# Four later modulation vectors of a two-layer transformer kernel: computed as four strips, turned in blocks, placed by sixteen transfers

## The chip, the cores and the metric

The kernel runs on one core of one Trainium2 chip. The time is device time in microseconds (us) of one execution. Three runs of the kernel before gave 2197.56, 2198.17 and 2198.8 us; their median is 2198.17 us. The core has a matrix engine (TensorE, called PE in the profile; its weight loads are PEld), a vector engine (VectorE, DVE), a scalar engine (ScalarE, ACT), a general engine (GpSimd, POOL) and a queue engine (SyncE, SP) that here issues all data transfers. Each engine takes its instructions in the order of the program and waits on semaphores for the others.

## The reference

Sixteen sequences x of 256 tokens by 256 features pass through two transformer layers, all in float32. Each layer has self-attention, cross-attention on a context, and a feed-forward part, each on a normalized input that is scaled and shifted by vectors computed from a condition of 256 features per sequence. These vectors are the modulations:

```python
def _adaln(x, c, lw, lb, gw, gb, bw, bb):          # layer 0
    g = (c @ gw + gb)[:, None, :]
    bt = (c @ bw + bb)[:, None, :]
    return _ln(x, lw, lb) * (1.0 + g) + bt
...
mod = jax.nn.silu(time_emb) @ Wmod + bmod          # layer 1, time_emb is the same condition
sh1, sc1, sh2, sc2, sh3, sc3 = jnp.split(mod, 6, axis=-1)
h = _ln(x, ln1_w, ln1_b) * (1 + sc1[:, None, :]) + sh1[:, None, :]
```

Layer 0 has two modulations (one shared by its two attentions, one for the feed-forward part), layer 1 has three. Each is a product of 16 conditions by a 256 x 512 weight: shift and scale, 256 features each.

## The kernel before

**Phases and jobs.** Six phases run one after another (self-attention, cross-attention and feed-forward of layer 0, then the same of layer 1). Each has 16 jobs, one per sequence `b`. An attention job has two steps `s`, a feed-forward job four. The order of every engine's instructions is that in which the Python code emits them (`manual_schedule`), so what stands in a step's code is also the order in each engine's queue; buffers are handed out by tile pools, which add the waits for a buffer's earlier readers. The main loop is at L901.

**A layer-0 attention step.** PE computes queries and keys of the next step (L82; for cross-attention also L502) into banks 0 to 3 of its accumulator. DVE multiplies them by the cosine and sine tables (`m`, L523), two tiles for each half: one under the tag `m0` and one under `m1`, two buffers each. POOL combines them to rotated queries and keys (`qk`, L531). PE multiplies these to scores (L566): first the half that goes into banks 0 to 3, then the half that goes into banks 4 to 7. ACT takes exponentials (`pr`, L578). DVE sums these (`both` L587, `squares` L593, `rows` L600). PE multiplies them with the values (L635, into banks 4 and 5), and ACT copies the products out (`raw`, L642). POOL divides by the sums (`raw`, L624) and makes the combinations for a product with seven instead of eight blocks (`folded`, L733). In the second step of a job PE forms the output of the previous job from these (`finish_folded`, banks 4 and 5) and DVE adds it to x (L747 to L754). DVE then normalizes a later job (`xh` L335, `blocks` L345), and its block transposes travel through DRAM (`turned` L350, `fetched` L360).

**Modulations.** The five products are called a1, a2 (layer 0) and b1, b2, b3 (layer 1). a1 and a2 use `modulation` (L180): eight products with a 128 x 128 weight block as the stationary operand and the 16 columns of `condT` as the moving one (L186), which leaves features on partitions, as `factors` (L165) needs them. `factors` are five small DVE instructions (L173 to L177) on 128 x 32 elements. a1 is made before the first job. a2 is made at `b == 2`, `s == 1` of the cross-attention phase (L923, L985), in the middle of the next step's rotary work, and its factors follow at once. b1, b2 and b3 are made at jobs 2, 5 and 8 of layer 0's feed-forward phase (L960) by `modulation_turned` (L192): the condition is the stationary operand (16 columns), the whole 256 x 512 weight passes in two products of 512 columns (L198). The result has conditions on partitions; POOL zeroes a 32 x 512 tile (L202), ACT copies the result into it (L203), DVE transposes it in 32 x 32 blocks (L205, tile `blocks`, tag `m1`; the tile `flat` has tag `m0`), and four transfers put the blocks on their partitions (L208, tile `turned`). The factors are made one job later (`at["mod"]()`, in step 3 of jobs 3, 6 and 9).

Of the kernel before, what the change touches and what calls it, by code (L numbers as in the profile page):

```python
# [10 lines left out]
F32 = mybir.dt.float32  # L11
# [5 lines left out]
P = 128  # L17
N = 256
D = 256
# [5 lines left out]
KC = D // P  # L25
# [18 lines left out]
def fast(ctx: ExitStack, tc: tile.TileContext, a: dict, out: bass.AP, flag):  # L44
# [4 lines left out]
    nc = tc.nc  # L49
    NB = a["x"].shape[0]  # L50
    assert NB >= 11

    const = ctx.enter_context(tc.tile_pool(name="const", bufs=1))
    resid = ctx.enter_context(tc.tile_pool(name="resid", bufs=1))
    wpool = ctx.enter_context(tc.tile_pool(name="wpool", bufs=2))
    work = ctx.enter_context(tc.tile_pool(name="work", bufs=2))
# [7 lines left out]
    def bank(i, *inner):  # L64

        flat = banks[:, i, :]
        if len(inner) == 1:
            return flat[:, 0 : inner[0]]
        return flat[:, 0 : inner[0] * inner[1]].rearrange("p (a n) -> p a n", n=inner[1])
# [34 lines left out]
    row_of, n_rows = {}, 0  # L104
# [17 lines left out]

    cond = work.tile([NB, D], F32, tag="m1", name="cond")
    nc.sync.dma_start(out=cond, in_=a["cond_1024"])
    condT = const.tile([P, 2, KC, NB], F32, name="condT")

    def transpose_condition(s, src):
        pc = bank(5 + s, KC, NB)
        for c in range(KC):
            nc.tensor.transpose(pc[:, c, :], src[:, c * P : (c + 1) * P], ident[:NB, :NB])  # L130
        nc.vector.tensor_copy(condT[:, s], pc)

    def idle_products(n):

# [5 lines left out]
    def condition():  # L140

        sig = work.tile([NB, D], F32, tag="inv", name="sig")
        nc.scalar.activation(sig, cond, AF.Sigmoid)
        soon = stat.tile([NB, 1], F32, tag="ve", name="soon")
        nc.scalar.activation(soon, cond[:, 0:1], AF.Exp)
        silu = work.tile([NB, D], F32, tag="inv", name="silu")
        idle_products(1)
        transpose_condition(0, cond)
        nc.vector.tensor_mul(silu, sig, cond)
        idle_products(1)  # L150
        transpose_condition(1, silu)
        idle_products(2)
        pr = bank(4, n_rows)
        nc.tensor.transpose(pr, rows, ident[:n_rows, :n_rows])
        return pr

    def load_modulation(shift_w, scale_w, name, between=None):
        w = wpool.tile([P, KC, 2, D], F32, tag="mod", name=f"mod_{name}", bufs=1)
        nc.sync.dma_start(out=w[:, :, 0, :], in_=shift_w.rearrange("(c p) m -> p c m", p=P))
        if between is not None:  # L160
            between()
        nc.sync.dma_start(out=w[:, :, 1, :], in_=scale_w.rearrange("(c p) m -> p c m", p=P))
        return w

    def factors(name, pm, ln_w, ln_b, shift_b, scale_b):  # L165


        factor = stat.tile([P, KC, NB], F32, tag="fac", name=f"fac_{name}", bufs=4)
        addend = stat.tile([P, KC, NB], F32, tag="add", name=f"add_{name}", bufs=4)
        ln_w, ln_b, shift_b, scale_b = (  # L170
            cols[:, c : c + KC].unsqueeze(2).to_broadcast([P, KC, NB]) for c in (ln_w, ln_b, shift_b, scale_b)
        )
        nc.vector.tensor_tensor(addend, pm[:, 1], scale_b, ALU.add)  # L173
        nc.vector.scalar_tensor_tensor(factor, addend, 1.0, ln_w, ALU.add, ALU.mult)
        nc.vector.scalar_tensor_tensor(addend, addend, 1.0, ln_b, ALU.add, ALU.mult)
        nc.vector.tensor_tensor(addend, addend, shift_b, ALU.add)
        nc.vector.tensor_tensor(addend, pm[:, 0], addend, ALU.add)  # L177
        return factor, addend

    def modulation(name, at, w, *vectors):  # L180

        pm = bank(at, 2 * KC, NB).rearrange("p (s c) b -> p s c b", s=2)
        for s in range(2):
            for m in range(KC):
                for k in range(KC):
                    nc.tensor.matmul(  # L186
                        pm[:, s, m, :], w[:, k, s, m * P : (m + 1) * P], condT[:, 0, k, :],
                        start=(k == 0), stop=(k == KC - 1),
                    )
        return factors(name, pm, *vectors)  # L190

    def modulation_turned(name, at, w, *vectors):  # L192


        assert NB <= 32
        pm = bank(at, 2 * D)[0:NB]
        for k in range(KC):
            nc.tensor.matmul(  # L198
                pm, condT[:, 1, k, :], w[:, k].rearrange("p s m -> p (s m)"), start=(k == 0), stop=(k == KC - 1)
            )  # L200
        flat = work.tile([32, 2 * D], F32, tag="m0", name=f"flat_{name}")
        nc.gpsimd.memset(flat, 0.0)  # L202
        nc.scalar.copy(flat[0:NB], pm)  # L203
        blocks = work.tile([32, 2 * KC, 4, 32], F32, tag="m1", name=f"blocks_{name}")
        nc.vector.transpose(blocks.rearrange("p s q b -> p (s q b)"), flat)  # L205
        turned = work.tile([P, 2, KC, NB], F32, tag="inv", name=f"turned_{name}")
        for q in range(4):
            nc.sync.dma_start(  # L208
                out=turned[32 * q : 32 * q + 32].rearrange("p s c b -> p (s c) b"), in_=blocks[:, :, q, 0:NB]
            )  # L210
        return lambda: factors(name, turned, *vectors)

    def layer0_modulation(i, between=None):
        w = load_modulation(a[f"L0_xcond_b{i}_w"], a[f"L0_xcond_g{i}_w"], f"a{i}", between)
        return lambda at: modulation(
            f"a{i}", at, w,
            *(row_of[f"L0_xcond_{n}"][0] for n in (f"ln{i}_w", f"ln{i}_b", f"b{i}_b", f"g{i}_b")),
        )

    def layer1_modulation(i):  # L220
        at = 2 * (i - 1) * D
        w = load_modulation(
            a["L1_xcond_Wmod"][:, at : at + D], a["L1_xcond_Wmod"][:, at + D : at + 2 * D], f"b{i}"
        )
        c = row_of["L1_xcond_bmod"][0] + at // P
        return lambda at: modulation_turned(
            f"b{i}", at, w, row_of[f"L1_xcond_ln{i}_w"][0], row_of[f"L1_xcond_ln{i}_b"][0], c, c + KC
        )


# [559 lines left out]
    def count_outside():  # L790
# [10 lines left out]
    phases = [  # L801
        {"layer": 0, "kind": "attn", "cross": False, "load": lambda part: load_layer0_attention("sa", part, load_first),
         "mod_load": lambda: layer0_modulation(1, lambda: load_x(0))},
        {"layer": 0, "kind": "attn", "cross": True, "load": lambda part: load_layer0_attention("ca", part), "mod_load": None},
        {"layer": 0, "kind": "ffn", "cross": False, "mod_load": lambda: layer0_modulation(2),
         "load": lambda part: load_ffn("L0_xcond_ff_w1", "L0_xcond_ff_w2", "L0_xcond_ff_b1", "L0_xcond_ff_b2", "a", part)},
        {"layer": 1, "kind": "attn", "cross": False, "load": load_layer1_self, "mod_load": lambda: layer1_modulation(1)},
        {"layer": 1, "kind": "attn", "cross": True, "load": load_layer1_cross, "mod_load": lambda: layer1_modulation(2)},
        {"layer": 1, "kind": "ffn", "cross": False, "mod_load": lambda: layer1_modulation(3),
         "load": lambda part: load_ffn("L1_xcond_W1", "L1_xcond_W2", "L1_xcond_b1", "L1_xcond_b2", "b", part)},  # L810
    ]
# [18 lines left out]
    for p, ph in enumerate(phases):  # L830
        for b in range(NB):
            job = {"phase": ph, "p": p, "layer": ph["layer"], "kind": ph["kind"], "cross": ph["cross"], "b": b,
                   "key": f"{p}_{b}", "index": len(jobs), "qk": {}, "pr": {}, "turns": [], "raw": [], "parts": [], "halves": [],
                   "last": p == len(phases) - 1}
# [66 lines left out]
    for i, (j, s) in enumerate(steps):  # L901
        job = jobs[j]
        ffn, layer0 = job["kind"] == "ffn", job["layer"] == 0
# [17 lines left out]
            load_phase(job["p"] + 1, "first")  # L921
        if layer0 and not ffn and s == 1 and job["b"] == 2:
            make_mod = phases[job["p"] + 1]  # L923

        if ffn and layer0 and job["b"] in (2, 5, 8):
            at = phases[3 + job["b"] // 3]
# [4 lines left out]
        if ffn and layer0 and job["b"] in (3, 6, 9) and s == 3:  # L931
            at = phases[2 + job["b"] // 3]
# [84 lines left out]
        else:  # L1017
            then = attention(i + 1, 1)
            at = 4 * s
# [639 lines left out]
```

## Time and profile before

| quantity | value |
|---|---|
| median of three runs | 2198.17 us |
| the profiled execution's own time | 2198.01 us |
| its span in the profile | 2196.1 us |
| PE busy | 2181.5 us (99%) |
| DVE busy | 1669.3 us (76%) |
| POOL busy | 1072.3 us (49%) |
| ACT busy | 838.2 us (38%) |
| four transfers of one modulation (L208), issue | 2.56 us (b1), 3.55 us (b2), 2.54 us (b3) |

The span begins with the first instruction and ends with the last; about 1.9 us of the execution's time lie outside it. In a timeline each line gives the start, the duration of the group, the engine, the line of the code, the operation, output and inputs, shapes and the number of records. One float32 product shows as two records on PE. "SPq" is the time in which SP issues a transfer, not the time the data takes. Idle time before a group is given in brackets with what ended it.

### The profile page before, as it was taken

Reading aid. Unit: us, or ns where it says so; the run is one execution under the profiler, and the core shown is the slowest. Engines: PE = TensorE matmul, PEld = TensorE weight load, DVE = VectorE, ACT = ScalarE, POOL = GpSimd, SP = SyncE. Lnnn points to the kernel's source line nnn. Section 1 sums busy time; section 2 is a strip of 40 time slices with the busy share of each in tenths; the row PEclk is TensorE's granted clock in tenths of the full one; section 3 lists DMA queues with packets and bytes.
Section 4 is the critical chain, followed back from the end, with each engine's and each line's share of the span. In section 5 each row is a group of like instructions: output and inputs, shape, how many; then the busy total and the mean of one; then the engine's idle time right before and its main releaser. Section 6 shows DMA issues by size and latency. Waiting matters only on the chain.

```text
span 2196.1 us, 110711 instructions
## 1 busy us (share of the span) xinstructions
PE 2181.5 (99%) x50469; PEld 1437.0 (65%) x50469; DVE 1669.3 (76%) x3119; ACT 838.2 (38%) x1306; POOL 1072.3 (49%) x1036
## 2 busy tenths in 40 slices
PE   9999999999999999999999999999999999999998
PEld 5656656656656666666666668787656656557887
DVE  6877777777787999989898876664777777777654
ACT  3323323323323333333333332334666666663222
POOL 3766566566557767676776752221323232222220
PEclk9999999999999999999999999999999999999999
DMA  6210111110132221212212033221222232223221
GB/s 192 49 37 23 27 37 23 28 37 22 31 89 64 71 60 35 59 41 45 56 37 60 23 74 87 52 45 29 62 43 42 52 95 59 62 52 85 61 62 37
DMA packets 307974, 117.77 MB, mean 54 GB/s; under 512 B 244308, under 2 KB 290728, under 8 KB 307368
## 3 DMA queue, kind: packets, MB, share of 16 engines
q1 hardware_dynamic: 307496, 110.61, 21.5%
q8 instruction: 396, 6.49, 1.3%
q14 instruction: 82, 0.67, 0.1%
HBM read 77.14 MB, written 33.29 MB: 50 GB/s over the span
## 4 chain that ended last, share of the span: by engine, by line
PE 92%; DVE 2%; POOL 2%; DMA 1%; issue 1%; SPq 1%; ACT 0%; DVEq 0%; POOLq 0%; ACTq 0%
PE banks L82 60%; PE banks L566 15%; PE banks L635 9%; PE banks L651 5%; PE banks L502 1%; PE banks L469 1%; POOL raw L624 1%; DVE m L523 1%; POOL qk L531 1%; DMA spread<-sums_seen 0%; POOL folded L733 0%; DMA turned<-blocks 0%; SPq L615 0%; DVE both L587 0%; SPq L350 0%
## 5 line engine op out<-in xcount | busy, mean ns | idle before, releaser
L578 ACT ACTIVATE pr<-banks 128x1024 f32<-128x1024 f32 x576 | 487.6, 938 | 414.3 <-PE banks L566 209.5
L531 POOL TENSOR_TENSOR qk<-m,m 128x512 f32<-128x512 f32 x256 | 347.0, 1376 | 292.5 <-DVE m L523 190.7
L523 DVE TENSOR_TENSOR m<-banks,rope 128x512 f32<-128x512 f32 x512 | 324.1, 679 | 87.1 <-POOL qk L531 83.2
L587 DVE TENSOR_TENSOR both<-pr 128x512 f32<-128x512 f32 x256 | 227.9, 903 | 101.4 <-ACT pr L578 101.2
L642 ACT COPY raw<-banks 128x512 f32<-128x512 f32 x128 | 75.0, 587 | 468.5 <-PE banks L635 461.8
L566 PE MATMUL banks<-qk 32*64 32x256 f32 x8192 | 241.3, 378 | 2.9 <-DVE x L750 2.0
L635 PE MATMUL banks<-pr,v 128*32 128x256 f32 x4096 | 233.2, 379 | 0.0
L566 PEld LDWEIGHTS banks<-qk 32*64 32x64 f32 x8192 | 185.4, 131 | 62.9 <-issue 23.0
L701 ACT ACTIVATE g<-banks,cols 128x256 f32<-128x256 f32 x256 | 106.9, 470 | 288.3 <-PE banks L82 274.9
L635 PEld LDWEIGHTS banks<-pr,v 128*32 128x32 f32 x4096 | 133.1, 110 | 88.5 <-ACT pr L578 0.7
L624 POOL TENSOR_TENSOR raw<-raw,spread 128x512 f32<-128x512 f32 x128 | 164.6, 1318 | 25.4 <-DMA spread<-sums_seen 23.2
L82 PE MATMUL banks<-folded_w,folded 128*32 128x128 f32 x5856 | 175.1, 273 | 0.4 <-POOL folded L733 0.3
L82 PEld LDWEIGHTS banks<-folded_w,folded 128*32 128x32 f32 x5856 | 162.5, 110 | 1.5 <-POOL folded L733 1.5
L593 DVE STREAM_TRANSPOSE squares<-both 128x1024 f32<-128x1024 f32 x128 | 159.4, 1246 | 4.4
L600 DVE TENSOR_REDUCE rows<-squares 128x32 f32<-128x1024 f32 x128 | 155.5, 1215 | 2.2
L686 POOL TENSOR_TENSOR oT<-oT,spread 128x256 f32<-128x256 f32 x64 | 45.7, 735 | 209.9 <-DVE spread L685 209.9
L327 POOL TENSOR_TENSOR rstd<-ve,neg_half 128x2 f32<-128x2 f32 x95 | 75.1, 790 | 144.0 <-DVE ve L325 140.7
L651 PE MATMUL banks<-pr,wide_v 128*32 128x256 f32 x2048 | 134.4, 379 | 1.1 <-ACT pr L578 1.1
L82 PE MATMUL banks<-hT,wk_sa 128*32 128x256 f32 x2048 | 134.9, 381 | 0.1
L420 POOL TENSOR_TENSOR x<-x,bo_b 128x256 f32<-128x256 f32 x96 | 73.1, 781 | 126.1 <-DVE xh L335 126.1
L82 PE MATMUL banks<-hT,wq_sa 128*32 128x256 f32 x2048 | 134.0, 379 | 0.0
L82 PE MATMUL banks<-hT,wq_ca 128*32 128x256 f32 x2048 | 133.9, 379 | 0.0
(157 smaller groups left out, 3669.6 us busy)
## 6 DMA issues: line engine op xcount, KB each, us to landing
turned<-blocks SPq DMA_DIRECT2D x380, 64.0 KB
fetched<-turned SPq DMA_DIRECT2D x380, 64.0 KB
spread<-sums_seen SPq DMA_DIRECT2D x128, 128.0 KB
x<-in_x SPq DMA_DIRECT2D x16, 256.0 KB
fetched_c<-turned_c SPq DMA_DIRECT2D x64, 64.0 KB
cT<-in_ctx_turned SPq DMA_DIRECT2D x16, 256.0 KB
out<-x SPq DMA_DIRECT2D x16, 256.0 KB
ctx<-in_ctx SPq DMA_DIRECT2D x16, 192.0 KB
```

What stands on the lines that cost most here:

```text
L82: nc.tensor.matmul(out[cut], lhsT[:, cut], rhs, start=start, stop=stop)
L523: nc.vector.tensor_tensor(m, pq, rope[:, s : s + 1, :].to_broadcast([P, 2, N]), ALU.mult)
L531: nc.gpsimd.tensor_tensor(r, x, y, (ALU.subtract, ALU.add)[out])
L566: nc.tensor.matmul(banks[64 * g : 64 * g + 64, at + h, t * N : (t + 1) * N], lhs, rhs, start=(half == 0), stop=(half == 1 or job["layer"] ...
L578: nc.scalar.activation(pr[:, one], sc[:, one], AF.Exp, scale=0.125 if job["layer"] == 0 else 0.25)
L587: nc.vector.tensor_tensor(job["both"][:, 2 * p : 2 * p + 2, :], pr[:, :, 0, :], pr[:, :, 1, :], ALU.add)
L593: nc.vector.transpose(job["squares"].rearrange("p b k -> p (b k)"), job.pop("both").rearrange("p h n -> p (h n)"))
L600: nc.vector.tensor_reduce(job["rows"][:, u, :], job.pop("squares"), AX.X, ALU.add)
L624: nc.gpsimd.tensor_tensor(part, part, spread[:, u : u + 1, :].to_broadcast([P, 2, N]), ALU.mult)
L635: nc.tensor.matmul(o[32 * h : 32 * h + 32, half, :], v[:, t, col : col + 32], prs[h // 2][:, h % 2, t, :], start=(t == 0), stop=(t == NT - 1),
L651: nc.tensor.matmul(o[32 * h : 32 * h + 32], v[:, t, 4 * c + h, 32 * e : 32 * e + 32], prs[h // 2][:, h % 2, t, :], start=(t == 0), stop=(t ...
L701: nc.scalar.activation(g[:, c, :], ph[:, c, :], AF.Gelu, bias=column(w["b1"], 2 * u + c))
```

## The change

All modulations but a1 are made by a new form of `modulation_turned`. `condT` is held with 32 columns, the last 16 zero. The product is cut into four pieces of 128 weight columns (shift and scale, two chunks each), and each piece goes to its own 32 partitions of the accumulator: eight products of 32 stationary and 128 moving columns instead of two of 16 and 512. The result is then a full 128 x 128 tile, so the zeroing on POOL falls away; ACT copies 128 x 128 elements, DVE transposes 128 x 128 elements in 32 x 32 blocks, and each of the sixteen blocks is put in place by a transfer of its own (32 partitions by 16 elements) instead of four blocks by one. a2 now goes this way too, at the same place in the step; its factors move from that place to the beginning of `b == 3`, `s == 1`, one job later. `condT` is zeroed once on POOL at the start.

```diff
-    condT = const.tile([P, 2, KC, NB], F32, name="condT")
+    assert NB <= 32
+    condT = const.tile([P, 2, KC, 32], F32, name="condT")
+    nc.gpsimd.memset(condT, 0.0)
...
-        nc.vector.tensor_copy(condT[:, s], pc)
+        nc.vector.tensor_copy(condT[:, s, :, 0:NB], pc)
...
-    def modulation_turned(name, at, w, *vectors):
-        assert NB <= 32
-        pm = bank(at, 2 * D)[0:NB]
+    def modulation_turned(name, of, at, w, *vectors):
+        pm = bank(at, P)
         for k in range(KC):
-            nc.tensor.matmul(
-                pm, condT[:, 1, k, :], w[:, k].rearrange("p s m -> p (s m)"), start=(k == 0), stop=(k == KC - 1)
-            )
-        flat = work.tile([32, 2 * D], F32, tag="m0", name=f"flat_{name}")
-        nc.gpsimd.memset(flat, 0.0)
-        nc.scalar.copy(flat[0:NB], pm)
-        blocks = work.tile([32, 2 * KC, 4, 32], F32, tag="m1", name=f"blocks_{name}")
-        nc.vector.transpose(blocks.rearrange("p s q b -> p (s q b)"), flat)
+            for g in range(4):
+                nc.tensor.matmul(
+                    pm[32 * g : 32 * g + 32], condT[:, of, k, :], w[:, k, g // KC, g % KC * P : (g % KC + 1) * P],
+                    start=(k == 0), stop=(k == KC - 1),
+                )
+        flat = work.tile([P, P], F32, tag="m0", name=f"flat_{name}")
+        nc.scalar.copy(flat, pm)
+        blocks = work.tile([P, 4, 32], F32, tag="m1", name=f"blocks_{name}")
+        nc.vector.transpose(blocks.rearrange("p q b -> p (q b)"), flat)
         turned = work.tile([P, 2, KC, NB], F32, tag="inv", name=f"turned_{name}")
         for q in range(4):
-            nc.sync.dma_start(
-                out=turned[32 * q : 32 * q + 32].rearrange("p s c b -> p (s c) b"), in_=blocks[:, :, q, 0:NB]
-            )
+            for g in range(4):
+                nc.sync.dma_start(
+                    out=turned[32 * q : 32 * q + 32, g // KC, g % KC, :], in_=blocks[32 * g : 32 * g + 32, q, 0:NB]
+                )
         return lambda: factors(name, turned, *vectors)
 
     def layer0_modulation(i, between=None):
...
-        return lambda at: modulation(
+        make = modulation if i == 1 else lambda name, *rest: modulation_turned(name, 0, *rest)
+        return lambda at: make(
...
+        if layer0 and not ffn and s == 1 and job["b"] == 3:
+            late_mod = phases[job["p"] + 1]
+            if late_mod["kind"] == "ffn":
+                late_mod["mod"] = late_mod["mod"]()
```

`modulation` (for a1) reads `condT[:, 0, k, 0:NB]` instead of `condT[:, 0, k, :]`, and `layer1_modulation` passes `of = 1`.

More of the change, by code (lines that the diff above doesn't have):

```diff
@@ L186, in modulation @@
                     nc.tensor.matmul(
-                        pm[:, s, m, :], w[:, k, s, m * P : (m + 1) * P], condT[:, 0, k, :],
+                        pm[:, s, m, :], w[:, k, s, m * P : (m + 1) * P], condT[:, 0, k, 0:NB],
                         start=(k == 0), stop=(k == KC - 1),
@@ L226, in layer1_modulation @@
         return lambda at: modulation_turned(
-            f"b{i}", at, w, row_of[f"L1_xcond_ln{i}_w"][0], row_of[f"L1_xcond_ln{i}_b"][0], c, c + KC
+            f"b{i}", 1, at, w, row_of[f"L1_xcond_ln{i}_w"][0], row_of[f"L1_xcond_ln{i}_b"][0], c, c + KC
         )
```

## The prediction

> **What bounds the kernel now.** I read the busy times, the slices and the chain of waits first. The page says:
>
> ```profile
> span 2196.1 us, 110711 instructions
> PE 2181.5 (99%) x50469; PEld 1437.0 (65%) x50469; DVE 1669.3 (76%) x3119; ACT 838.2 (38%) x1306; POOL 1072.3 (49%) x1036
> DVE  6877777777787999989898876664777777777654
> PE 92%; DVE 2%; POOL 2%; DMA 1%; issue 1%; SPq 1%; ACT 0%; DVEq 0%; POOLq 0%; ACTq 0%
> ```
>
> PE sets the time, but around slices 13 to 22 (cross-attention of layer 0, where a2 is made) DVE is as full as PE, and its in-order queue can stop PE. So I read two stretches of the timeline. First PE in the feed-forward phase, at the same product of successive jobs:
>
> ```profile
> 1351.28 1.99 PE L82 MATMUL banks<-w_a,folded 128*32 128x128 f32 x63
> 1364.30 1.99 PE L82 MATMUL banks<-w_a,folded 128*32 128x128 f32 x63
> 1378.82 0.40 PE L82 MATMUL banks<-w_a,folded 128*32 128x128 f32 x6
> 1392.06 1.99 PE L82 MATMUL banks<-w_a,folded 128*32 128x128 f32 x63
> ```
>
> A job takes 13.02 us (1364.30 - 1351.28); the two that hold b2 take 27.76, so b2 costs PE 27.76 - 26.04 = 1.72 us, all of it in the time. Then the step in which a2 is made:
>
> ```profile
> 787.16 1.96 PE L186 MATMUL banks<-condT,mod_a 128*128 128x16 f32 x16
> 789.05 0.64 PE L82 MATMUL banks<-cT,wk_ca 128*32 128x256 f32 x8
> 790.13 2.56 POOL L531 TENSOR_TENSOR qk<-m,m 128x512 f32<-128x512 f32 x2 [0.72 <-DVE add_a L173]
> 790.35 1.16 DVE L175 SCALAR_TENSOR_TENSOR add_a<-add_a,cols 128x32 f32<-128x32 f32 x1
> 791.54 1.21 DVE L176 TENSOR_TENSOR add_a<-add_a,cols 128x32 f32<-128x32 f32 x1
> 794.41 2.47 DVE L523 TENSOR_TENSOR m<-banks,rope 128x512 f32<-128x512 f32 x4
> 802.52 0.42 DVE L754 TENSOR_TENSOR x<-banks,x 128x256 f32<-128x256 f32 x1
> 801.34 3.71 PE L566 MATMUL banks<-qk 32*64 32x256 f32 x128
> ```
>
> DVE ends its additions to x (they read banks 4 and 5) at 802.94; PE's second half of scores, which writes banks 4 to 7, begins at about 801.34 + 1.85 = 803.2. Between DVE and PE there are 0.25 us of slack, no more. The transfers of a modulation and, one job later, the place where the change puts a2's factors:
>
> ```profile
> L208 SPq DMA_DIRECT2D turned_b<-blocks_b x12: 591/602/1608, 1334.9 to 1418.3; - x12
> 1334.86 2.56 SPq L208 DMA_DIRECT2D turned_b<-blocks_b  x4
> 819.52 4.98 POOL L624 TENSOR_TENSOR raw<-raw,spread 128x512 f32<-128x512 f32 x4 [0.85 <-DMA spread<-sums_seen]
> 821.59 0.47 DVE L325 TENSOR_SCALAR ve_c<-mv_c 128x2 f32<-128x2 f32 x1
> 823.35 3.39 DVE L587 TENSOR_TENSOR both<-pr 128x512 f32<-128x512 f32 x2 [1.30 <-ACT pr L578]
> 824.58 4.55 POOL L733 TENSOR_TENSOR folded<-raw,raw 128x512 f32<-128x512 f32 x3
> ```
>
> An issue takes 0.60 us, one in twelve 1.6. And DVE waits for POOL: two `both` take 3.39 us instead of some 0.6 each.
>
> **What the Trainium skill says.** "SBUF — State Buffer", section "Who interferes with whom": a DVE instruction with two SBUF inputs and a GpSimd instruction that reads SBUF exclude each other for the whole instruction. The trace agrees: L175 ends at 791.51, as POOL's first qk does (790.13 + 1.28), L176 at 792.75, as its second does, though L173 and L177, which read a bank, take 0.17 and 0.19. "DMA: Bandwidth & Descriptors", "Queues, rings and completion order": only the completion count says that data has landed, so a buffer is free for reuse after that and not after the issue. The trace has 1.76 us from issue to use (`cond`: issued 0.72, used 2.48). "TensorEngine Tiling (Array Packing)", "Key Properties": tiles run independently, a switch of mode drains. The strip products here (64 records in 1.74 us, 795.12 to 796.86) agree: 27 ns per record of 128 columns, against 430 ns for one of 512.
>
> **The change, part by part.**
>
> *b1, b2, b3 on PE.* Before, 1.72 us each. After, 8 products are 16 records of 27 ns = 0.44 us. Saved 1.28 x 3 = 3.84 us, in a phase where PE alone sets the pace.
>
> *b1 to b3 elsewhere.* The POOL zeroing (0.51 us) goes, copy and transpose get shorter; none is on the path. SP issues 16 instead of 4: about 16 x 0.65 + 1.3 = 11.7 instead of 2.6 us. Behind them wait, for b1, four weight loads and the `fetched` transfers, which become some 8 us late; hT on ACT and POOL then comes up to 7 us late, but serves a job that begins a further 13 us on. The factors (1345.6, last block landed about 1346 to 1347) make DVE wait some 2 us; the next PE user of its folds comes 3 us after them (1364.30 against 1361.1 in the next job). Cost 0; if the cover is gone, 1 to 3 us once.
>
> *a2 on PE.* From scores to scores the step takes 21.61 us with it (779.73 to 801.34) and 19.59 one job later (820.18 to 839.77): 2.02 us for a2, 0.44 after. A gain of 1.58, unless DVE makes PE wait.
>
> *a2's new waits.* `flat` and `blocks` take `m0` and `m1` buffers between the two halves of the rotary work. `flat` waits for POOL's first qk (791.41). Then ACT's copy (0.20 for one element, 0.47 for 256: estimate 0.3), DVE's transpose (0.42 for 256 columns: estimate 0.25) and hand-overs: first issue at about 792.05. DVE did the factors here until 792.97, so up to this point it loses nothing. But the last of the following four `m` instructions, the sine part of the second half, takes the `m1` buffer that `blocks` held; it waits until all sixteen transfers have landed. Pitch of an issue 0.65: the last is issued at 792.05 + 15 x 0.65 = 801.8; 1.3 slow issues in sixteen add 1.3; landing adds 1.76: 804.9. Before, this `m` began at 796.20. DVE stands still 8.8 us, and behind it, in order, are the reductions and the additions to x for which PE's banks 4 and 5 wait. Less the slack of 0.25: PE is 8.6 us later than before, the 1.58 already lost in it. POOL's qk, the exponentials and the next job shift along; PE has no idle time later to make it good. Bounds: a pitch of 0.42 (`spread`, its median) and no slow issue gives 800.1, PE +3.7; POOL's second qk first and two or three slow issues give 807, PE +10.7.
>
> *a2's factors.* Five instructions of 0.19 go from a place where DVE would have waited for POOL anyway to the one after `ve_c` (822.06). There DVE has 1.30 us idle, and 5 x 0.22 = 1.1 would fit: lower bound 0. But all five now read two SBUF operands, and POOL runs seven instructions back to back until 829.1. One DVE instruction gets through for each of POOL's: ends near 823.3, 824.6, 826, 827.5, 829, then two `both` until about 831 instead of 826.74. Upper bound 4.3 - 0.25 = 4.0. I take 3.5: the first may slip in. The delay passes through `m` (waiting for qk already) to the same additions to x.
>
> *Start.* A memset of `condT` on POOL at about 1.3 us (0.2, as for `ident`) lies before its first writer at 2.93: 0.
>
> Sum, against the profiled execution's 2198.01 (0.16 below the median): -3.84 + 8.6 + 3.5 = +8.3, so **2206.3 us**, span 2204.4.
>
> **Rivals.**
>
> A. The buffer waits as said, the factors fit into the idle 1.30 us: -3.84 + 8.6 = +4.8, 2202.8. For it: the mutual exclusion shows at only a few places. Against: it showed at 790 to 793 for these very instructions.
>
> B. Small transfers issue faster (0.42): -3.84 + 3.7 + 3.5 = +3.4, 2201.4. For: each has 32 rows, not 128. Against: transfers of 4 rows out of SBUF (`sums_seen` from `sums`) have a median of 573 ns.
>
> C. Faster: all of it hidden, only PE's gain remains: -3.84 - 1.58 = -5.4, 2192.6. The place is the `m1` buffer; it decides at a landing before 796.4, that is a pitch of (796.4 - 792.05 - 1.76) / 15 = 0.17 us per issue, and the shortest issue in the profile is 0.30. It also needs the factors hidden.
>
> D. The strips don't run side by side, since each has its own moving data: 16 x 0.107 = 1.7 us, no gain, +12.1, 2210.1. Against: L635 has different data in each strip and runs 64 records of 256 columns in 3.64 us.
>
> **How the numbers follow.** Forecast 62%, A 20%, B 9%, C 5%, D 4%. About 0.2% (4.4 us) is what a measurement can tell from no change, so slower begins at 2202.6. Slower: nearly all of the forecast, over half of A, all of D, a little of B: 0.79. Same: the rest of A and B: 0.16. Faster: C, 0.05. The range goes from a quick pitch with partly hidden factors (2200) to two or three slow issues and the full price of the factors (2211); for the forecast alone it is 2203.5 to 2210.
>
> **What would show it.** L200 with 16 records in about 0.45 us; 13.5 instead of 14.5 us for the job with a modulation; sixteen SP issues over 10 to 12 us from 792; one `m` (L527) with a DVE idle time of some 8 us ended by the DMA of `turned_a`; scores after it near 812 instead of 803; factors of a2 taking 5 to 7 us next to POOL's L628 and L737. I am wrong if that `m` waits under 4 us, if the factors take about 1 us, or if b1's late `fetched` stops PE.

## The result

The changed kernel takes 2206.3 us (median of 6 runs, 2205.26 to 2206.95) against 2197.88 us (6 runs, 2194.55 to 2198.8) of the kernel before on the same chip: a ratio of 1.0039, 95% interval 1.0026 to 1.0052. The forecast was 2206.3 us. A second set of runs gave 2207.37 us (5 runs) and the same ratio, 1.0039 (1.0025 to 1.0053). The profiled execution took 2205.66 us, its span is 2203.9 us.

### The profile page after: what moved, and what is told of

It reads as the page before. It is cut to its first block, busy times and chain, and to the rows that moved or that the text cites. A ratio compares the mean times of both kernels' runs of the same rounds, so it can differ in the third digit from the quotient of the medians.

```text
span 2203.9 us, 110835 instructions
## 1 busy us (share of the span) xinstructions
PE 2183.0 (99%) x50505; PEld 1454.6 (66%) x50505; DVE 1664.6 (76%) x3120; ACT 837.6 (38%) x1307; POOL 1073.0 (49%) x1034
## 4 chain that ended last, share of the span: by engine, by line
PE 95%; DVE 1%; POOL 1%; DMA 1%; issue 1%; SPq 1%; ACT 0%; DVEq 0%; POOLq 0%; ACTq 0%
PE banks L82 62%; PE banks L570 16%; PE banks L639 9%; PE banks L655 5%; PE banks L506 1%; PE banks L473 1%; POOL raw L628 1%; SPq L211 0%; DVE m L527 0%; POOL qk L535 0%; POOL folded L737 0%; DMA sums_seen<-inv 0%; DMA rows<-in_rows 0%; DVE squares L597 0%; DVE rows L604 0%
## 5 line engine op out<-in xcount | busy, mean ns | idle before, releaser
L591 DVE TENSOR_TENSOR both<-pr 128x512 f32<-128x512 f32 x256 | 222.1, 880 | 103.9 <-ACT pr L582 103.7
```

The lines of the kernel that those rows point to most:

```text
L591: nc.vector.tensor_tensor(job["both"][:, 2 * p : 2 * p + 2, :], pr[:, :, 0, :], pr[:, :, 1, :], ALU.add)
```

## The profile after

The page of the changed kernel, in the views shown of the kernel before (busy times, DVE's slices, shares of the chain of waits):

```profile
span 2203.9 us, 110835 instructions
PE 2183.0 (99%) x50505; PEld 1454.6 (66%) x50505; DVE 1664.6 (76%) x3120; ACT 837.6 (38%) x1307; POOL 1073.0 (49%) x1034
DVE  5877777777788979988988886664777777777664
PE 95%; DVE 1%; POOL 1%; DMA 1%; issue 1%; SPq 1%; ACT 0%; DVEq 0%; POOLq 0%; ACTq 0%
```

The page hides the loss: PE is busy 99% as before, and 1.5 us longer, though it was given some 5 us less to do (3.65 us at b1 to b3, 1.58 at a2). The answer is in the timeline. First the step in which a2 is made (columns as before: start, duration, engine, line, operation, records, and in brackets the idle time before it with what ended it):

```profile
787.22 0.62 PE L200 MATMUL banks<-mod_a,condT 128*32 128x128 f32 x16
791.43 0.27 ACT L205 COPY flat_a<-banks 128x128 f32<-128x128 f32 x1 [5.64 <-POOL qk L535]
791.73 0.31 DVE L207 STREAM_TRANSPOSE blocks_a<-flat_a 128x128 f32<-128x128 f32 x1 [1.76 <-ACT flat_a L205]
792.11 10.76 SPq L211 DMA_DIRECT2D turned_a<-blocks_a  x16
793.11 1.87 DVE L527 TENSOR_TENSOR m<-banks,rope 128x512 f32<-128x512 f32 x3
804.17 0.69 DVE L527 TENSOR_TENSOR m<-banks,rope 128x512 f32<-128x512 f32 x1 [9.19 <-DMA turned_a<-blocks_a]
804.91 3.26 PE L570 MATMUL banks<-qk 32*64 32x256 f32 x58 [4.34 <-DVE m L527]
810.05 0.61 PE L570 MATMUL banks<-qk 32*64 32x256 f32 x2 [1.88 <-DVE x L754]
810.98 2.54 PE L570 MATMUL banks<-qk 32*64 32x256 f32 x62 [0.31 <-DVE x L758]
813.44 1.99 PE L506 MATMUL banks<-cT,wk_ca 64*64 64x256 f32 x16
```

Three of the four `m` run at 793, the fourth 9.19 us later, when the last of the sixteen transfers has landed. It started at 796.20 before: 7.97 us, of which 0.17 was there when the step began. PE's first stop, of 4.34 us, waits for this `m` itself: it reads the banks that the first half of scores writes. Behind it on DVE stand the additions to x (L754, L758), for which PE waits twice more. One job later come a2's factors and the two `both` behind them, on DVE:

```profile
831.07 1.34 DVE L175 TENSOR_TENSOR add_a<-turned_a,cols 128x32 f32<-128x32 f32 x1
832.45 0.19 DVE L176 SCALAR_TENSOR_TENSOR fac_a<-add_a,cols 128x32 f32<-128x32 f32 x1
832.67 1.15 DVE L177 SCALAR_TENSOR_TENSOR add_a<-add_a,cols 128x32 f32<-128x32 f32 x1
833.86 1.21 DVE L178 TENSOR_TENSOR add_a<-add_a,cols 128x32 f32<-128x32 f32 x1
835.10 1.20 DVE L179 TENSOR_TENSOR add_a<-turned_a,add_a 128x32 f32<-128x32 f32 x1
836.23 1.32 DVE L591 TENSOR_TENSOR both<-pr 128x512 f32<-128x512 f32 x2
```

L175 to L179 are the factors; they end at 836.30, about 5.2 us after the first began. But the two `both` take 1.32 us where they took 3.39 before.

In the feed-forward phase the same product of successive jobs starts at 1334.31, 1347.77, 1360.79, 1374.94 and 1388.39: the job with b1 takes 13.46 us, so a modulation costs PE 0.44 us. The job from 1360.79 to 1374.94 takes 14.15 us instead of 13.02. The queue of SP and what follows from it, in the timeline of the changed kernel:

```profile
1344.14 12.45 SPq L211 DMA_DIRECT2D turned_b<-blocks_b  x16
1356.63 0.58 SPq L275 DMA_DIRECT2D wqkv_b<-in_L_xcond_Wqkv  x1
1358.83 1.75 SPq L364 DMA_DIRECT2D fetched<-turned  x4
1364.62 0.60 ACT L397 ACTIVATE hT<-fetched,add_a,fac_a 128x256 f32<-128x256 f32 x1 [7.55 <-DMA fetched<-turned]
```

ACT waits 7.55 us for `fetched`, with the activations (`g`) queued behind. What PE loses in this job lies in one group of its products, the last of the feed-forward output:

```profile
1364.61 0.78 PE L82 MATMUL banks<-folded_w,folded 128*32 128x128 f32 x15
1366.03 2.26 PE L82 MATMUL banks<-folded_w,folded 128*32 128x128 f32 x74 [0.64 <-issue]
```

From its first record (1364.28) to the next job's products (1368.24) it takes 3.96 us, against 2.81 before (1341.75 to 1344.56). "<-issue" says that the profile names nothing that ended this stop. So the span has +9.3 us for the wait at a2 (scores of the step after: 820.18 before, 829.63 after, less 0.17), +1.25 for the factors (the product behind the scores one step on: 844.46 and 855.16), +1.13 for the stop after b1 and -3.65 for b1 to b3: +8.0, where the spans differ by 7.7.

## Experiments

The start of the first profile of the kernel before was a lucky one (see the first run below), and single executions differ by one to two us. So beside each time stand two stretches read from the traces, both free of the start. Stretch A runs from the reduction `rows` in the first step of cross-attention job 2 (775.54 before) to an addition to x in the feed-forward job that makes b1 (1330.44): it holds a2. Stretch B runs from there to an addition to x after b3 (1452.40). The last column is PE's second full job after b1, the one that took 14.15 us. Differences are against the first profile of the kernel before; there is one profile for each line.

```
                                  median   ratio to before (95%)     A        B       job
kernel before, again              2199.38  1.0001 (.9993-1.0010)    +0.73    +0.03   13.02
changed kernel                    2206.3   1.0039 (1.0026-1.0052)  +10.43    -2.55   14.15
changed kernel, again             2207.37  1.0039 (1.0025-1.0053)  +11.62    -2.37   14.33
a2 undone                         2195.34  0.9979 (.9971-.9988)     -0.28    -2.52   14.18
a2 with own buffers               2196.61  0.9988 (.9981-.9995)     -0.49    -3.29   13.41
own buffers, factors moved        2197.39  0.9992 (.9984-1.0001)    +4.53    -2.65   14.03
a2's transfers doubled            2217.78  1.0077 (1.0062-1.0093)  +21.65    -2.73   13.97
a2 undone, loads a job later      2195.19  0.9982 (.9975-.9989)     +0.11    -1.95   14.53
a2 undone, loads behind           2195.2   0.9985 (.9977-.9992)     -0.69    -3.47   13.02
a2 in self-attention, job later   2193.62  0.9973 (.9962-.9984)     -2.15    -3.48   13.02
a2 in self-attention, behind      2194.14  0.9978 (.9968-.9988)     -1.88    -3.47   13.02
PE turns, a2 in self-attention    2196.35  0.9987 (.9979-.9995)     -1.70    -2.26   13.02
```

**The kernel before, and the changed one, again.** How much of a difference is the execution, not the code?

> The kernel before, unchanged, for a second profile of it. All five profiles of kernels with the change in them are 1.1 to 3.5 us behind the first profile of the kernel before after the start (the third reduction of the first job), and most have lost that again by the cross-attention phase. If this is chance (when the granted TensorE clock rises in the first 12 us), this profile is 1 to 3.5 us behind the first one there too, and its time is the same as the kernel before. If it is the change (the zeroing of condT), this profile starts as the first one did.

The second profile of the same kernel is 3.4 us behind the first by the third reduction of job 0; a1's sixteen records take 3.53 us in it and 2.02 in the first. PE had its full clock from 15.5 us on in the second, from 6.4 us on in the first. So the slower start is chance. Between 0.8 and 2.5 us of such a lag are given back, in every profile, when the cross-attention phase begins; why was not tried.

> The changed kernel, unchanged, for a second profile of it. Theory: from the last job before a2 to the end of the cross-attention phase it is about 10.4 us later than the kernel before, as in its first profile (9.3 for the wait of m, 1.25 for the factors), and PE's granted clock falls to half for some microseconds right after the wait, as it did there and, for longer, with a2's transfers doubled. If the fall of the clock was chance, it is absent here and the stretch is about 1 us shorter.

Stretch A is +11.6, 1.2 more than in the first profile: this time `m` waited 10.08 us. The clock fell here too, to half from 804.71 to 811.53 and from 814.95 to 818.36; that it fell was not chance.

**a2 undone.** Is the loss a2's?

```diff
-        make = modulation if i == 1 else lambda name, *rest: modulation_turned(name, 0, *rest)
+        make = modulation
...
-            if late_mod["kind"] == "ffn":
-                late_mod["mod"] = late_mod["mod"]()
+            pass
```

> Only a2 is undone: it is made by the form of the kernel before (features on partitions, factors at once); b1, b2, b3 keep strips and sixteen transfers. Theory (all of the loss is a2's: 9.3 us buffer wait and 1.25 us factors, against 3.65 us gained on PE at b1 to b3 and 1.1 us lost once to b1's late fetched): -3.65 + 1.1 = -2.5 us against the kernel before, about 2195.5, some 10.5 us below the changed kernel. Rival (the sixteen transfers of b1 to b3 or the longer start cost as much as they gain): within 0.5 us of the kernel before, or above it.

Faster than the kernel before, by 0.21%: 2.6 to 6.4 us by the interval, where 2.5 was forecast. Stretch A is back to -0.28 and B keeps its -2.5, together 2.8 us, which the interval holds. All of the loss is in a2.

**Buffers of its own.** Which part of a2? The transfers stay; only what they hold is no longer wanted by `m`.

```diff
-        flat = work.tile([P, P], F32, tag="m0", name=f"flat_{name}")
+        own = name == "a2"
+        flat = work.tile([P, P], F32, tag="flat_own" if own else "m0", name=f"flat_{name}", bufs=1 if own else 2)
-        blocks = work.tile([P, 4, 32], F32, tag="m1", name=f"blocks_{name}")
+        blocks = work.tile([P, 4, 32], F32, tag="blocks_own" if own else "m1", name=f"blocks_{name}", bufs=1 if own else 2)
```

> The changed kernel, but flat and blocks of a2 have buffers of their own, so that no rotary m waits for the transfers; the sixteen transfers themselves, their queue and the place of the factors stay. Theory (the wait for the m1 buffer costs PE 9.3 us, and PE's own gain of 1.58 us at a2 shows once it is gone): no m with a DVE wait of 9 us, time -3.65 + 1.1 + 0.2 + 1.25 - 1.58 = -2.7 us against the kernel before, about 2195.3. Rival (the SP queue is what is late: sixteen issues of 10.8 us hold up the transfers behind them, so another wait takes the place of this one): 2200 to 2206.

The timeline of this kernel:

```profile
792.95 11.40 SPq L212 DMA_DIRECT2D turned_a<-blocks_a  x16
794.63 2.54 DVE L528 TENSOR_TENSOR m<-banks,rope 128x512 f32<-128x512 f32 x4 [1.18 <-POOL qk L536]
802.63 3.71 PE L571 MATMUL banks<-qk 32*64 32x256 f32 x128
```

SP issues for 11.40 us as before, yet all four `m` run in one piece and PE's 128 records of scores in one piece. The time is 2.9 us below the kernel before (forecast 2.7); stretch A falls from +10.4 to -0.49, where -1.58 + 1.25 = -0.33 was expected. The rival with SP's queue is out: it was the buffer.

**Transfers doubled.** Does the wait grow with the number of issues? Each block of a2 also goes to a tile that nobody reads.

```diff
+        places = [turned]
+        if name == "a2":
+            places.append(work.tile([P, 2, KC, NB], F32, tag="spare", name="spare", bufs=1))
...
-                nc.sync.dma_start(
-                    out=turned[32 * q : 32 * q + 32, g // KC, g % KC, :], in_=blocks[32 * g : 32 * g + 32, q, 0:NB]
-                )
+                for place in places:
+                    nc.sync.dma_start(
+                        out=place[32 * q : 32 * q + 32, g // KC, g % KC, :], in_=blocks[32 * g : 32 * g + 32, q, 0:NB]
+                    )
```

> The changed kernel, but each of a2's sixteen transfers is followed by one of the same block to a place that nobody reads, so that the m1 buffer is read by 32 transfers. Theory (m waits for the number of issues times their pitch of 0.65 to 0.67 us): the m waits 9.2 + 10.6 = 19.8 us, time +10.5 us against the changed kernel, about 2216.8. Rival (the wait is mostly the latency of landing, which transfers share): the m waits under 12 us, time under 2209.

Timeline (`m`, scores) and, in the last two lines, the windows view, whose columns are window, its length, busy time of PE, PEld, DVE, ACT and POOL with their instructions, the clock granted to PE (1.00 is full), share of DMA, GB/s:

```profile
816.57 0.69 DVE L531 TENSOR_TENSOR m<-banks,rope 128x512 f32<-128x512 f32 x1 [20.48 <-DMA spare<-blocks_a]
817.32 3.70 PE L574 MATMUL banks<-qk 32*64 32x256 f32 x58 [15.92 <-DVE m L531]
...
809.00:816.00 7.00, 0.00 (x0) 0.00 (x0) 0.00 (x0) 0.00 (x0) 0.00 (x0) 0.50 0.04 3
816.00:822.00 6.00, 3.70 (x58) 1.97 (x58) 5.33 (x7) 0.90 (x1) 2.50 (x2) 0.53 0.00 0
```

The wait is 20.5 us instead of 9.2 (forecast 19.8): 0.70 us for each of the sixteen more, slow ones included. From the first issue to the last it is 20.83 us instead of 10.17, so 10.7 of the 11.3 us more are issuing and 0.6 landing.

This run also shows what the clock does behind the wait. It falls to half at 804.57, within the stop, and is full again at 821.64; the second half of scores finds it full:

```profile
823.38 1.98 PE L574 MATMUL banks<-qk 32*64 32x256 f32 x62 [0.31 <-DVE x L762]
```

In the changed kernel the same 62 records take 2.54 us. So the scores of the step after begin 23.89 us behind that `m` here, 25.46 us in the changed kernel and 23.98 us in the kernel before.

**Factors moved.** Can the factors' 1.25 us be saved where DVE waits for POOL anyway? Starting from the kernel with own buffers:

```diff
-        if layer0 and not ffn and s == 1 and job["b"] == 3:
-            late_mod = phases[job["p"] + 1]
-            if late_mod["kind"] == "ffn":
-                late_mod["mod"] = late_mod["mod"]()
...
                 sum_up(late, 6)
+            if s == 1 and job["b"] == 3:
+                late_mod = phases[job["p"] + 1]
+                if late_mod["kind"] == "ffn":
+                    late_mod["mod"] = late_mod["mod"]()
```

> As the one with own buffers, and a2's five factors at b == 3, s == 1 move from the head of the step to the place behind the first half of the rotary work, where DVE waits for POOL's qk in any case. Theory (at the head of the step they cost PE 1.25 us): 1.2 us less than with own buffers alone, about 2194.1. Rival (the 1.25 us is a shift that later slack gives back, or the factors delay m at the new place as much): the same as with own buffers alone, within 0.4 us.

Both theories missed: stretch A went from -0.49 to +4.53. The timeline of this kernel, POOL and DVE:

```profile
830.69 2.57 POOL L536 TENSOR_TENSOR qk<-m,m 128x512 f32<-128x512 f32 x2
830.90 1.16 DVE L177 SCALAR_TENSOR_TENSOR add_a<-add_a,cols 128x32 f32<-128x32 f32 x1
832.10 1.21 DVE L178 TENSOR_TENSOR add_a<-add_a,cols 128x32 f32<-128x32 f32 x1
833.21 2.52 POOL L738 TENSOR_TENSOR folded<-raw 128x512 f32<-128x512 f32 x2
833.34 1.20 DVE L179 TENSOR_TENSOR add_a<-turned_a,add_a 128x32 f32<-128x32 f32 x1
834.46 1.81 DVE L592 TENSOR_TENSOR both<-pr 128x512 f32<-128x512 f32 x1
836.20 2.47 DVE L528 TENSOR_TENSOR m<-banks,rope 128x512 f32<-128x512 f32 x4
```

The exclusion named in the prediction holds one for one: L177 and L178 end with POOL's two `qk`, L179 and `both` go with its two `folded`. The four `m` start at 836.20, though the first `qk`, for which they wait elsewhere, was done at 830.69 + 1.29 = 831.98. There was no free wait: DVE waits 1.2 us for POOL there, and four instructions with two SBUF operands need four of POOL's. Of the 5.0 us against own buffers alone, 3.3 are this later start of `m` (behind the start of stretch A). The rest follows a stop of PE, after which its clock was half from 845.53 to 848.95:

```profile
843.87 0.61 PE L571 MATMUL banks<-qk 32*64 32x256 f32 x2 [3.17 <-DVE x L755]
844.79 3.06 PE L571 MATMUL banks<-qk 32*64 32x256 f32 x62 [0.31 <-DVE x L759]
```

The 62 records take 3.06 us instead of 1.98, L507 behind them 1.64 instead of 1.09. At the head of the step the `both` would have paid for the exclusion in any case.

**The weight loads.** What makes `fetched` late at b1, and does PE stop for it? Starting from the kernel with a2 undone, the four early loads were moved first one job on (`b == 4` instead of `3`, not shown), then one step on, behind the `fetched` transfers of the same job:

```diff
-        if s == 1 and job["b"] == (3 if ffn else 1) and more:
+        if s == (2 if ffn else 1) and job["b"] == (3 if ffn else 1) and more:
```

> As the one with a2 undone, but the four early weight loads of the layer after are issued one job later, so that b1's late fetched transfers do not also stand behind them on SP. Theory (the 2.2 us of weight-load issues are what makes hT and with it PE 1.1 us late, once): the job after b1 takes PE 13.0 instead of 14.15 us, time 1.1 us less than with a2 undone alone, about -3.7 us against the kernel before. Rival (PE's 1.1 us there is from the factors or from ACT's copy, not from the transfers): that job stays at 14.1 us and the time is that with a2 undone alone.

A miss: the job takes 1.5 us too long instead of 1.1. The loads now stand ahead of the next four `fetched` transfers. These (timeline) are issued from 1354.51 to 1356.32, and hT starts at 1362.09, 5.8 us after the last issue. But PE runs again at 1361.17, before hT. And with a2 in the self-attention phase the loads stand at the same place ("job later" in the table) without any stop.

> As the one with a2 undone, but the four early weight loads of the layer after are issued one step later, behind the fetched transfers instead of ahead of them. Theory (PE stops for 0.4 to 1.5 us in the job after b1 because the data of the fetched transfers lands 4 to 6 us after its issue when 1.3 MB of weights have been issued just ahead of it, and under 2 us without them): that job takes PE 13.0 us, time 1.1 us less than with a2 undone alone. Rival (the sixteen transfers alone make fetched late enough): that job stays above 13.4 us.

With the loads behind, the timeline shows

```profile
1333.54 11.89 SPq L211 DMA_DIRECT2D turned_b<-blocks_b  x16
1345.55 2.30 SPq L364 DMA_DIRECT2D fetched<-turned  x4
1349.54 0.60 ACT L397 ACTIVATE hT<-fetched,add_a,fac_a 128x256 f32<-128x256 f32 x1 [3.07 <-DMA fetched<-turned]
1350.60 0.62 SPq L275 DMA_DIRECT2D wqkv_b<-in_L_xcond_Wqkv  x1
```

hT starts 1.7 us after the last issue of `fetched` (1347.85), against 4.0 us in the changed kernel (1360.58 to 1364.62). The job takes 13.02 us, stretch B reads -3.47 us, near the 3.65 that PE gains. So `fetched` is late where the weights' data (1.3 MB) stand ahead of it, and in this run PE's stop is gone. In times, the 1 us doesn't show (2195.34 and 2195.2).

That PE stops because `fetched` is late is not shown. In the profiles with such a stop (the changed kernel twice, a2 undone, factors moved, transfers doubled, loads a job later) PE runs again anywhere from 0.9 us before to 1.4 us after hT starts. One other thing fits all of them. The DMA view of the kernel before has a queue of instructions:

```profile
q8 instruction: 396, 6.49, 1.3%
```

These are 396 packets of 16 KB, 64 bytes for each of the 100,938 records of PE and PEld, so they look like PE's own instructions. In the six profiles PE runs again 1.2 to 1.4 us after the end of such a packet, and that packet came late: it began 7.1 to 8.5 us after the one before it, when most of the weights' data had passed (5.5 us with the loads behind, where PE did not stop). Over all thirteen profiles, each of the fourteen stops of PE over 0.25 us without a releaser, between 60 and 2150 us, ends 1.2 to 1.5 us after a packet of this queue. So the likelier reading is that PE ran out of instructions, because the weights' data were ahead of them; no run tried it.

**a2 in the self-attention phase.** Is a2's new form worth anything where PE alone sets the pace? The loads and products of a2 go to jobs 1 and 2 of the first phase, its factors to job 3, with own buffers. The early loads are moved as above, one job on in the first kernel and behind `fetched` in the second.

```diff
-        if layer0 and not ffn and s == 1 and job["b"] == 2:
-            make_mod = phases[job["p"] + 1]
...
+        if job["p"] == 0 and s == 1 and job["b"] == 2:
+            make_mod = phases[2]
+        if job["p"] == 0 and s == 1 and job["b"] == 3:
+            phases[2]["mod"] = phases[2]["mod"]()
```

> All modulations but a1 in the new form with their sixteen transfers, but a2 is made in the self-attention phase (b == 2, factors at b == 3 there) with buffers of its own, and the early weight loads are issued one job later. Theory (the cost of the sixteen transfers and of the factors lies only in what waits for them in the DVE-bound cross-attention phase; PE sets the pace of the self-attention phase alone): PE -3.65 for b1 to b3 and -1.58 for a2, nothing else: -5.2 us against the kernel before. Rival (the factors next to POOL cost PE in any step, or SP's ten microseconds make fetched late here too): -3.5 us or less of a gain.

> All modulations but a1 in the new form with sixteen transfers, a2 in the self-attention phase with buffers of its own, the early weight loads one step later, behind the fetched transfers. Theory: no stop of PE at b1, no wait for the m1 buffer: -5.2 us against the kernel before, the same as with the loads one job later, since that run had no stop either. Rival (what moved a2 saves in the cross-attention phase it costs in the self-attention phase): -3.5 us or less of a gain.

The two differ only in where the early loads stand. They take 2193.62 and 2194.14 us, 0.27% (0.16 to 0.38) and 0.22% (0.12 to 0.32) below the kernel before: the first is the fastest version here, though its interval overlaps that of a2 undone. Stretch A loses a2's 2.02 us (-2.15, -1.88); the self-attention phase gets 0.9 to 1.0 us longer, where 0.44 was expected. What the other 0.5 us is was not tried.

**PE turns the result.** The transfers can be left out altogether: one product with the identity turns 128 x 128 elements. The identity is then kept for the whole run, and `flat` has a buffer of its own.

```diff
-        blocks = work.tile([P, 4, 32], F32, tag="m1", name=f"blocks_{name}")
...
-        return lambda: factors(name, turned, *vectors)
+        def turned(at):
+            pt = bank(at, P)
+            nc.tensor.transpose(pt, flat, ident)
+            return factors(
+                name, pt.rearrange("p (s c b) -> p s c b", s=2, b=32)[:, :, :, 0:NB], *vectors
+            )
+        return turned
```

> The strips stay, but instead of DVE's turn in blocks and the sixteen transfers, PE turns the 128 x 128 result in one transpose, one job later, and the factors read the bank; a2 is made in the self-attention phase. Theory (a transpose of 128 x 128 takes PE 0.27 us, as those of xh at the start do; no transfer, no late fetched): b1 to b3 3 x (1.72 - 0.44 - 0.27) = 3.0, a2 2.02 - 0.71 = 1.3: -4.3 us against the kernel before. Rival (a transpose between the strips drains PE and costs it over 1 us, or a bank is waited for): no gain over the kernel before.

It is 0.13% (0.05 to 0.21) faster than the kernel before, less than forecast. The transposing job costs PE 0.40 us, not 0.27 (13.42 us instead of 13.02), and 0.78 us at b1. And the self-attention phase gets 2.7 us longer, where 0.71 was expected; 1.27 us of it is a stop of PE (to 90.72) without a releaser.

## Why the prediction was right

**b1 to b3 on PE: right.** 13.46 - 13.02 = 0.44 us each, as forecast; 3.65 us in all against 3.84, because b1's old form had cost 1.53 us and not 1.72 (27.57 us for its two jobs). Rival D is out.

**a2's wait: right in place and mechanism, the sum right by two errors.** `m` began at 804.17, forecast 804.9: the last issue began at 802.3, since slow issues added 0.4 us to 792.11 + 15 x 0.65 and not 1.3 (the longest took 0.99 us), and the data was there 1.9 us later (1.76 forecast). The pitch was 0.68 us, so rivals B and C are out. That is a delay of 7.8 us, and it passed through the additions to x as forecast. (The forecast has a slip: 804.9 - 796.20 is 8.7, so less the slack 8.45, not 8.6.) PE lost 9.3, because of a cost that the sum lacked: its granted clock fell twice (windows view of the changed kernel; the column after POOL is the clock):

```profile
800.00:805.00 5.00, 0.66 (x14) 0.21 (x19) 0.83 (x2) 0.00 (x0) 0.00 (x0) 1.00 0.04 4
805.00:809.00 4.00, 3.17 (x58) 1.83 (x58) 3.93 (x5) 0.77 (x1) 2.50 (x2) 0.57 0.00 0
812.00:816.00 4.00, 4.00 (x66) 1.73 (x54) 3.93 (x8) 1.94 (x2) 2.05 (x4) 0.57 0.42 69
```

The first fall is hidden, since PE waits for x afterwards anyway. The second slows the scores and what follows: L506 takes 1.99 us instead of 1.09, 62 records of scores 2.54 us, 1.98 at full clock. That is the missing 1.5 us; with the transfers doubled there is no second fall, and it is not lost. The Trainium skill, "TensorE: Matmul & The Clock Gate", section "What's actually happening", halves the clock after an idle window of about 3.4 us. I had not taken that page into the sum. The first fall agrees in this profile (PE idle from 800.57 to 804.91, half clock from 805.44) and nearly with the transfers doubled (idle from 801.40, half clock from 804.57); in the second profile of the changed kernel it came after only 2.1 us (802.56 and 804.71). The second fall, which costs the time, has no such idle window before it: the stops were 1.88 and 0.31 us, and with the transfers doubled stops of 1.44 and 0.31 us brought none. Its cause stays open; no run kept PE busy through the wait.

**a2's factors: wrong in size.** Forecast 3.5 us, measured 1.25 on PE. The five did take 5.2 us, four of them one for one with POOL. What the step left out is that the two `both` behind them no longer paid for the exclusion: 1.32 us instead of 3.39. Rival A (they fit into idle time) was no better: it had them free by being short. On DVE the factors cost more than on PE. Its reductions `rows` lag behind the kernel before by 7.8 us after the wait, 8.6 in the step after it and 10.6 after the factors; with the transfers doubled by 19.4, 19.4 and 21.5; with own buffers by -2.6, -2.1 and 0.0. So DVE is set back 2.0 to 2.1 us by the factors each time and 0.8 by the clock. In the changed kernel PE had lost part of that to the clock already, so its 9.3 and 1.25 are one split of 10.55 us, against 12.1 forecast, and not two costs that stand alone.

**b1's late `fetched`: wrong.** The step said 0, with 1 to 3 us if the cover is gone, and it named a stop of PE there as a sign of being wrong. PE did stop, for 1.13 us. But that it stopped for `fetched` isn't shown; its stops fit late packets of instructions better (see the weight loads). The sum had no term for what else stands behind 1.3 MB of weights. And the lateness of `fetched` was underestimated: issued behind these weights, its data was used 4 to 6 us after the last issue, not 1.8.

**Start: right as far as it can be told**, since the start varies by 3 us from execution to execution.

The errors (+0.7 at the wait, -2.25 at the factors, +1.13 at b1, +0.2 each at PE's gain and the start) cancel; the exact hit is luck. The direction and the main term aren't: own buffers take away the wait, and with it the loss.

## What to carry over

A product made four times cheaper on PE can still lose if its result travels in sixteen transfers through a buffer that the vector engine needs next: count issues times pitch (0.65 to 0.70 us here), and give a small result a buffer of its own. Ask what stands behind the waiting instruction on each engine's queue, and what a burst of weights holds up on the way in, PE's instructions perhaps among it. Move such work into a phase in which only PE is full.

## What the runs showed of the hardware

- Stops of PE of 3.2 us and more in the cross-attention phase came with half clock: one of 4.3 us with two spells of 3.4 us, one of 5.6 us with spells of 6.8 and 3.4 us, one of 3.2 us with one of 3.4 us. One of 15.9 us had half clock for 17.1 us, most of it within the stop, and no second spell. Each of these spells is 3.41 us or a multiple of it.
- A transfer of 32 partitions by 64 bytes out of SBUF takes SP 0.59 us to issue, some of them 0.9 to 1.8 us; the four of `fetched` (1.75 us together) take 0.44 us each.
- Data of the four `fetched` transfers out of DRAM was used 1.7 us after the last issue, and 4.0 to 5.8 us after it when four weight loads stood right ahead of them.
- All fourteen stops of PE over 0.25 us for which the profiles name no releaser end 1.2 to 1.5 us after a 16 KB packet of an instruction queue.
- Five DVE instructions of 0.19 us with two SBUF operands take 4.1 to 5.2 us beside a busy POOL; whether that costs anything depends on whether the instructions behind them would have waited as well.
